# The node stage of a graph layer: one product in its own loop, tokens kept transposed, a written order, first gathers ahead of a branch

## The chip, the core and the metric

The kernel runs on one core of a Trainium2 chip. The core has TensorE (matmuls; PE, its weight loads PEld), VectorE (DVE), ScalarE (ACT) and GpSimd (POOL), which work side by side on on-chip memory (SBUF, and PSUM for the matmuls' sums), and SyncE (SP), which issues transfers. Each engine works through its own queue in order and waits for the others by semaphores. The metric is the device time of one execution in microseconds; lower is better.

## The reference

Two layers work on 6250 nodes of 256 features and 100000 edges. The change lies where layer 0 ends and layer 1 (a graph attention layer) begins. Cut to that:

```python
x = x + processed                                  # layer 0's FFN, for the chosen half of the nodes
xn = layer_norm(layer_norm(x), ln1_g, ln1_b)
h = (xn @ W).reshape(N, HEADS, HEAD_DIM)
a_src = einsum('nhd,hd->nh', h, att_src)
a_dst = einsum('nhd,hd->nh', h, att_dst)
e = leaky_relu(a_src[src] + a_dst[dst], 0.2)
alpha = softmax of e over the edges of each dst
agg = segment_sum(h[src] * alpha[:, :, None], dst)
out = agg.reshape(N, 256) + xn @ W_res + bias
out = layer_norm(out, ln2_g, ln2_b)
...
```

Behind it come a dense FFN of 1024 hidden units and a mixture of eight experts.

## The kernel before

**Tiles.** The 6250 nodes are 50 tiles of 125 (`NT`, `NP`). X, the nodes' features, stays in SBUF for the whole run. Edges are sorted by destination; each node tile has 17 columns of 128 edges (`SL`), in three groups of six, six and five (`GS`).

**The node stage (lines 589 to 695)** runs between layer 0 and layer 1's edges. For every tile:
- `mix` on VectorE adds layer 0's FFN output Y, weighted by wm, to X (L613), and takes mean and variance (bn_stats L177, aggregate L178). `rs` then makes inverse roots for a whole span of tiles by 12 small instructions (L166 to L172); L617 makes the offset. The spans are 1, 2, 2 and then nine times 5 tiles: 12 in all.
- `front`: z = X normalised (ScalarE, L623), two transposes of z on TensorE (L627), and two activations that apply gain and offset and write xT (ScalarE, L629).
- two products of xT on TensorE: with W and the attention vectors into ph, 272 columns (L651), and with W_res into pr, 256 columns (L653).
- three evictions: ht (ScalarE, L654), the attention terms ASAD (VectorE, L655), and rr = pr + bias (VectorE, L656). Per span ht is stored to the table htab and rr to rtab, both in HBM, on SP's queue (L84), and the greatest attention terms of the span go into ext (L660 to L665).

The order of the instructions on each engine is chosen by a scheduler here, which lets instructions of several tiles stand between one another.

**From the stage to the edges.** A few small instructions make one flag of ext (L671 to L692). `nc.values_load(f1I)` (L698) reads it on every engine, and a branch (L699) skips the general path, which these inputs don't need. The load waits for every engine's work and every transfer that is under way. Behind the branch VectorE makes adsh, the destinations' terms in three bf16 parts (L709 to L717). Then the edge part begins: `fetch(s)` gathers a group's rows of htab, one indirect DMA of 128 rows for each column, on GpSimd (L342), into a ring of four buffers, and for a tile's third group SP reads the tile's own rows (L752, L753). `fetch_tile(t)` has SP read the tile's one-hot source ohT (L759, 535 KB) and rr. `load` has SP read expert weights (L146). `onehot_t` compares ohT (VectorE, L766), `spread` multiplies it by adsh (TensorE, L774), and `quarter0` to `quarter3` do a group's softmax weights, the weighted rows and their sum in four quarters; L812 is the first instruction of a group's first quarter. From L723 on, the order on TensorE, VectorE and ScalarE is the program's own, with quarters of the edge work put between the products of FFN and experts of the nodes that are done.

At L1138 the edge part starts with `load(0)`, `load(1)`, `fetch(0)`, `fetch_tile(0)`, `fetch(1)`, `fetch(2)`. GpSimd's only other work here is in `add_o`: L916 adds a constant row to X, 14 times in all, and is placed by the scheduler in the node stage, behind each chunk's last z, since it needs nothing later.

Of the kernel before, what the change touches and what calls it, by code (L numbers as in the profile page):

```python
# [58 lines left out]
def gnn_ffn(ctx, tc, A, out):  # L59
# [529 lines left out]
    w2 = ctx.enter_context(tc.tile_pool(name="w2", bufs=1))  # L589
    with ExitStack() as md:  # L590
# [6 lines left out]
        for t0 in range(0, NT, XC):  # L597
            Y.append(wp.tile([NP, XC, D], F32, name=f"Y{t0}"))
            ndma(Y[-1], ytab, t0, True, eng=(nc.sync, nc.scalar)[(t0 // XC) % 2])
# [5 lines left out]
        MC = 5  # L605
        spans = [(0, 1), (1, 2), (3, 2)] + [(t, MC) for t in range(5, NT, MC)]

        def mix(t0, c):

            mv = pool.tile([NP, MC, 2], F32, name="mv")  # L610
            for j in range(c):
                t = t0 + j
                nc.vector.scalar_tensor_tensor(X[:, t, :], Y[t // XC][:, t % XC, :], wm[:, t:t + 1], X[:, t, :], op0=ALU.mult, op1=ALU.add)  # L613
                bn(pool, mv[:, j, :], X[:, t, :])
            r2 = pool.tile([NP, 2, MC], F32, name="r2", bufs=3)
            rs(pool, r2[:, 0, 0:c], mv[:, 0:c, 1], 1.0 + 1e-5, 1e-10)
            nc.vector.scalar_tensor_tensor(r2[:, 1, 0:c], mv[:, 0:c, 0], -1.0, r2[:, 0, 0:c], op0=ALU.mult, op1=ALU.mult)  # L617
            return r2

        def front(t, r2, j):  # L620

            z = pool.tile([NP, D], F32, name="z")
            nc.scalar.activation(z, X[:, t, :], AF.Identity, bias=r2[:, 1, j:j + 1], scale=r2[:, 0, j:j + 1])  # L623
            pt = psum.tile([P, KD, NP], F32, name="mi", bufs=3)
            xT = pool.tile([P, KD, NP], F32, name="xT", bufs=3)
            for k in range(KD):
                nc.tensor.transpose(pt[:, k, :], z[:, k * P:(k + 1) * P], ident[0:NP, 0:NP])  # L627
            for k in range(KD):
                nc.scalar.activation(xT[:, k, :], pt[:, k, :], AF.Identity, bias=ln1_b[:, k:k + 1], scale=ln1_g[:, k:k + 1])  # L629
            return xT  # L630

        stats = [mix(*spans[0])]
        fronts = []
        for s, (t0, c) in enumerate(spans):
            if s + 1 < len(spans):
                stats.append(mix(*spans[s + 1]))
            if s == 0:
                fronts.append(front(0, stats[0], 0))
            ht = pool.tile([NP, MC, HW], F32, name="ht")
            rr = pool.tile([NP, MC, D], F32, name="rr")  # L640
            for j in range(c):
                t = t0 + j
                if j + 1 < c:
                    fronts.append(front(t + 1, stats[s], j + 1))
                elif t + 1 < NT:
                    fronts.append(front(t + 1, stats[s + 1], 0))
                xT = fronts[t]
                ph = psum.tile([NP, HA], F32, name="ph")
                pr = psum.tile([NP, D], F32, name="pr")
                for k in range(KD):  # L650
                    nc.tensor.matmul(ph, xT[:, k, :], wcat[:, k, 0:HA], start=(k == 0), stop=(k == KD - 1))  # L651
                for k in range(KD):
                    nc.tensor.matmul(pr, xT[:, k, :], wcat[:, k, HA:HA + D], start=(k == 0), stop=(k == KD - 1))  # L653
                nc.scalar.activation(ht[:, j, :], ph[:, 0:HW], AF.Copy)  # L654
                nc.vector.tensor_copy(ASAD[:, t, :], ph[:, D:HA])  # L655
                nc.vector.tensor_tensor(rr[:, j, :], pr, g_bias[0:NP, :], ALU.add)  # L656
            ndma(ht[:, 0:c, :], htab, t0, False)
            ndma(rr[:, 0:c, :], rtab, t0, False)
            e1 = pool.tile([NP, MC, 2 * HEADS], F32, name="e1")
            nc.vector.tensor_copy(e1[:, 0:c, 0:HEADS], ASAD[:, t0:t0 + c, 0:HEADS])  # L660
            nc.vector.tensor_scalar(e1[:, 0:c, HEADS:], ASAD[:, t0:t0 + c, 0:HEADS], -1.0, None, op0=ALU.mult)
            e2 = ext if s == 0 else pool.tile([NP, 2 * HEADS], F32, name="e2")
            nc.vector.tensor_reduce(e2, e1[:, 0:c, :].rearrange("p t h -> p h t"), AX.X, ALU.max)
            if s:
                nc.vector.tensor_tensor(ext, ext, e2, ALU.max)  # L665
# [30 lines left out]

        mid.close()
# [9 lines left out]


        rem = keep.tile([NP, NT, 2 * HEADS], F32, name="rem")  # L709
        for ts in (slice(0, 3), slice(3, NT)):  # L710
            nc.vector.tensor_tensor(shift[:, ts], shift[:, ts], ASAD[:, ts, HEADS:], ALU.add)
            leaky(rem[:, ts, HEADS:], shift[:, ts])
            nc.vector.tensor_copy(rem[:, ts, 0:HEADS], ASAD[:, ts, HEADS:])
            for q in range(3):
                nc.vector.tensor_copy(adsh[0:NP, ts, q, :], rem[:, ts])
                if q < 2:
                    nc.vector.tensor_tensor(rem[:, ts], rem[:, ts], adsh[0:NP, ts, q, :], ALU.subtract)  # L717
# [5 lines left out]
    with ExitStack() as p2:  # L723
        pool = p2.enter_context(tc.tile_pool(name="p2", bufs=2))
        wp = p2.enter_context(tc.tile_pool(name="w3", bufs=1))
        psum = p2.enter_context(tc.tile_pool(name="p2p", bufs=2, space=PSUM))
        p2.enter_context(tc.manual_schedule(engines={mybir.EngineType.PE, mybir.EngineType.DVE, mybir.EngineType.Activation}))

        imin = wp.tile([P, P], F32, name="imin")
        nc.vector.tensor_scalar_min(imin, iota, float(NP))  # L730
        selfT = wp.tile([NP + 1, P], BF16, name="selfT")
        nc.vector.tensor_scalar(selfT, imin[0:NP + 1, :], pcol[0:NP + 1, :], None, op0=ALU.is_equal)
        ring = [wp.tile([P, GS, HW], F32, name=f"hrow{k}") for k in range(4)]
        for r in ring:
            nc.gpsimd.memset(r[:, GS - 1, :], 0.0)
        NG = -(-SL // GS)
        assert NG * GS == SL + 1
        LAST = NT * NG
        live, tiles, outs, ended = {}, {}, {}, set()
        place = {t0 + j: (c, j) for c, (t0, n) in enumerate(CHUNKS1) for j in range(n)}  # L740

        def fetch(s):
            if s >= LAST:
                return
            t, g = divmod(s, NG)
            rows = ring[s % len(ring)]
            live[s] = {"rows": rows}
            for i in range(GS):
                if g * GS + i < SL:
                    gather(rows[:, i, :], htab, srcT[:, t, g * GS + i:g * GS + i + 1])  # L750
                else:
                    nc.sync.dma_start(rows[0:SPLIT, i, :], htab[NP * t:NP * t + SPLIT, :])  # L752
                    nc.sync.dma_start(rows[SPLIT:NP, i, :], htab[NP * t + SPLIT:NP * (t + 1), :])  # L753
# [379 lines left out]
        def ends(ci):  # L1133

            t0, n = CHUNKS1[ci]
            return 4 * NG * (t0 + n) + 3

        load(0, ("W1", "W2", "Wo"))  # L1138
        load(1, ("W1", "W2"))
        fetch(0)  # L1140
        fetch_tile(0)
        for k in range(1, len(ring) - 1):
            fetch(k)
        onehot_t(0)
# [430 lines left out]
```

## Time and profile before

| | us |
|---|---|
| median of 3 runs | 3304.16 (3302.11 to 3304.63) |
| the profiled execution | 3303.96, of which its span 3302.2 |

| row of the page | count | busy us | mean ns |
|---|---|---|---|
| TensorE, L651 (ph) in the node stage | 200 | 56.7 | 406 |
| TensorE, L653 (pr) in the node stage | 200 | 52.3 | 385 |
| ScalarE, L629 (xT) | 100 | 40.0 | 452 |
| GpSimd, L916 | 14 | 29.9 | 2136 |
| ScalarE, L623 (z) | 50 | 29.6 | 593 |
| VectorE, L613 (mix) | 50 | 25.1 | 505 |
| VectorE, L656 (rr) | 50 | 20.7 | 414 |
| VectorE, L177 (bn_stats) | 50 | 20.6 | 416 |
| ScalarE, L654 (ht) | 50 | 19.2 | 384 |
| GpSimd, L342, gathers of htab over the whole run | 850 | 952.7 | 1121 |

These are the groups of instructions between 1258 and 1383 us of the span, and for the last row those of the page. An fp32 product counts twice per contraction half, so 50 tiles make 200 instructions. Busy times of one engine can add up to more than the time, as an instruction begins before the one ahead of it has ended; for what an engine gets through, the distance from start to start is the better number. Idle time of an engine counts only where something waits for it.

### The profile page before, as it was taken

Reading aid. Unit: us, or ns where it says so; the run is one execution under the profiler, and the core shown is the slowest. Engines: PE = TensorE matmul, PEld = TensorE weight load, DVE = VectorE, ACT = ScalarE, POOL = GpSimd, SP = SyncE. Lnnn points to the kernel's source line nnn. Section 1 sums busy time; section 2 is a strip of 40 time slices with the busy share of each in tenths; the row PEclk is TensorE's granted clock in tenths of the full one; section 3 lists DMA queues with packets and bytes.
Section 4 is the critical chain, followed back from the end, with each engine's and each line's share of the span. In section 5 each row is a group of like instructions: output and inputs, shape, how many; then the busy total and the mean of one; then the engine's idle time right before and its main releaser. Section 6 shows DMA issues by size and latency. Waiting matters only on the chain.

```text
span 3302.2 us, 40488 instructions
## 1 busy us (share of the span) xinstructions
PE 2842.7 (86%) x12746; PEld 1981.7 (60%) x12746; DVE 2011.5 (61%) x5670; ACT 1165.6 (35%) x2193; POOL 1857.6 (56%) x1772
## 2 busy tenths in 40 slices
PE   5378889888888996757889999999999999999999
PEld 5245666666666674546666666665666666666665
DVE  8543444444444459578777677767667777766731
ACT  5111212222222224534443534344353434434332
POOL 0277777777777741277665555556555555556300
PEclk8679999999999997979999999999999999999999
DMA  5633343333333426466454454535444454544312
GB/s 106 172 103 111 112 114 111 110 110 112 112 110 112 115 73 158 126 170 187 138 169 131 127 152 118 156 106 151 127 127 140 120 151 120 148 123 134 115 48 64
DMA packets 263978, 412.04 MB, mean 125 GB/s; under 512 B 55450, under 2 KB 202374, under 8 KB 263711
## 3 DMA queue, kind: packets, MB, share of 16 engines
q0 software_dynamic: 81600, 226.41, 24.7%
q1 hardware_dynamic: 169062, 170.03, 17.9%
q10 hardware_dynamic: 13080, 12.80, 1.6%
q8 instruction: 106, 1.74, 0.2%
q14 instruction: 130, 1.06, 0.1%
HBM read 376.61 MB, written 33.24 MB: 124 GB/s over the span
## 4 chain that ended last, share of the span: by engine, by line
PE 29%; DVE 9%; issue 7%; POOL 6%; DMA 3%; ACT 3%; DVEq 0%; POOLq 0%; ACTq 0%
PE ph L1021 14%; PE py L1039 7%; POOL hrow L342 6%; PE py L934 3%; PE iotaP L835 3%; DMA hrow<-htab,sdT 2%; DVE lo L800 2%; DVE hrow L843 1%; DVE ad L812 1%; DVE X L1042 1%; DVE bnst L177 1%; PE ph L923 1%; PE pa L774 1%; PE mi L961 1%; ACT h L1022 1%
## 5 line engine op out<-in xcount | busy, mean ns | idle before, releaser
L342 POOL DMA_INDIRECT hrow<-htab,sdT x850 | 952.7, 1121 | 681.3 <-DVE lo L800 319.9
L342 POOL DMA_INDIRECT rows<-gtab,sdT x850 | 805.7, 948 | 258.5 <-issue 128.6
L404 PE MATMUL ps<-rows,oh 128*125 128x257 f32 x1700 | 479.2, 421 | 76.4 <-DMA rows<-gtab,sdT 62.8
L1022 ACT ACTIVATE h<-ph,bi,sc 128x500 f32<-128x500 f32 (+3 forms) x448 | 322.4, 722 | 600.8 <-PE ph L1021 600.4
L404 PEld LDWEIGHTS ps<-rows,oh 128*125 128x125 f32 x1700 | 326.3, 203 | 218.0 <-DMA rows<-gtab,sdT 130.9
L1021 PE MATMUL ph<-h,W 128*128 128x500 f32 (+3 forms) x896 | 380.3, 557 | 0.6 <-ACT h L1022 0.6
L1021 PE MATMUL ph<-wcat,W 128*128 128x500 f32 (+3 forms) x896 | 373.8, 557 | 0.3
L1039 PE MATMUL py<-Wo,h 128*125 128x256 f32 x1600 | 370.9, 381 | 0.4 <-ACT h L1022 0.4
L800 DVE TENSOR_TENSOR lo<-hrow,hi 128x792 fp32r<-128x792 f32 (+1 forms) x300 | 296.0, 987 | 119.0 <-ACT hi L853 119.0
L1039 PEld LDWEIGHTS py<-Wo,h 128*125 128x125 f32 x1600 | 297.5, 188 | 72.4 <-issue 26.1
L1042 DVE SCALAR_TENSOR_TENSOR X<-py,gate,X 125x256 f32<-125x256 f32 x400 | 174.8, 480 | 221.8 <-PE py L1039 220.3
L843 DVE TENSOR_TENSOR hrow<-hrow 128x768 f32<-128x768 f32 x300 | 273.0, 952 | 32.6 <-ACT hrow L821 32.4
L853 ACT ACTIVATE hi<-hrow 128x792 fp32r<-128x792 f32 (+1 forms) x300 | 232.4, 817 | 144.3 <-DVE hrow L843 144.1
L835 PE MATMUL iotaP<-hi,oh 128*125 128x264 f32 x850 | 252.9, 329 | 0.0
L1021 PEld LDWEIGHTS ph<-wcat,W 128*128 128x128 f32 x896 | 166.2, 198 | 143.3 <-issue 120.1
L835 PE MATMUL iotaP<-lo,oh 128*125 128x264 f32 x850 | 224.1, 295 | 31.3 <-DVE lo L800 31.2
L1021 PEld LDWEIGHTS ph<-h,W 128*128 128x128 f32 x896 | 162.4, 197 | 109.6 <-issue 98.1
L835 PEld LDWEIGHTS iotaP<-lo,oh 128*125 128x125 f32 x850 | 163.5, 192 | 50.8 <-DVE lo L800 37.3
L467 PE MATMUL ph<-xT,f_w 128*128 128x500 f32 (+3 forms) x448 | 189.9, 549 | 0.5 <-ACT xT L457 0.5
L923 PE MATMUL ph<-xT,h_w 128*128 128x500 f32 (+3 forms) x448 | 184.0, 555 | 1.9 <-ACT hT L925 1.0
L476 PE MATMUL py<-f_w,hT 128*125 128x256 f32 x800 | 182.8, 381 | 1.2 <-DVE y L477 0.4
L934 PE MATMUL py<-h_w,hT 128*125 128x256 f32 x800 | 177.6, 380 | 0.0
(305 smaller groups left out, 3706.2 us busy)
## 6 DMA issues: line engine op xcount, KB each, us to landing
W<-in_L_ffn_W SPq DMA_DIRECT2D x224, 256.0 KB
Wo<-in_L_ffn_Wo SPq DMA_DIRECT2D x112, 256.0 KB
ohT<-dltab SPq DMA_DIRECT2D x50, 535.5 KB
rows<-gtab,sdT POOLq DMA_INDIRECT x850, 2.8
hrow<-htab,sdT POOLq DMA_INDIRECT x850, 3.3
hrow<-htab SPq DMA_DIRECT2D x50, 115.5 KB
X<-in_x ACTq DMA_DIRECT2D x10, 560.0 KB
ytab<-y SPq DMA_DIRECT2D x50, 112.0 KB
```

The source lines that it names most:

```text
L342: nc.gpsimd.indirect_dma_start(out=dst, out_offset=None, in_=tab, in_offset=bass.IndirectOffsetOnAxis(ap=idx, axis=0))
L404: nc.tensor.matmul(ps, oh[:, i, :], rows[:, i, :], start=(s0 + i == 0), stop=(s0 + i == SL - 1))
L800: nc.vector.tensor_tensor(L["lo"][:, c], L["rows"][:, c], L["hi"][:, c].bitcast(F32), ALU.subtract)
L835: nc.tensor.matmul(tiles[t]["ps"], L["oh"][:, i, :], r[:, i, :], start=(g + i + q == 0), stop=(g * GS + i == SL - 1 and q == 1))
L843: nc.vector.tensor_tensor(h4, h4, rows[:, c, D:, None].to_broadcast([P, GS // 2, HEADS, HD]), ALU.mult)
L853: nc.scalar.activation(L["hi"][:, c], L["rows"][:, c], AF.Copy)
L923: nc.tensor.matmul(ph[:, 0:n], h_w1[:, k, f * P:(f + 1) * P], C["xT"][:, k, 0:n], start=(k == 0), stop=(k == KD - 1))
L934: nc.tensor.matmul(py[:, i, :], C["hT"][f][:, j * NP:(j + 1) * NP], h_w2[:, f, :], start=(f == 0), stop=(f == NF - 1))
L1021: nc.tensor.matmul(ph[:, 0:n], w[:, k, f * P:(f + 1) * P], rhs[:, k, 0:n], start=(k == 0), stop=(k == KD - 1))
L1022: nc.scalar.activation(h[:, f, 0:n], ph[:, 0:n], AF.Relu, bias=cols[1][:, f, e:e + 1], scale=cols[0][:, f, e:e + 1])
L1039: nc.tensor.matmul(py[:, i, :], hidden[u, "2"][:, k, j * NP:(j + 1) * NP], weights[u, "Wo"][:, k, :], start=(k == 0), stop=(k == KD - 1))
L1042: nc.vector.scalar_tensor_tensor(X[:, t0 + j, :], py[:, i, :], chunk[ci]["gate"][:, j, e:e + 1], X[:, t0 + j, :], op0=ALU.mult, op1=ALU.add)
```

## The change

The node stage is written anew; the rest of the program stays as it is.

- The W_res product leaves the tile's trip and gets a loop of its own behind the table's. For that the transposed tokens of all 50 tiles stay on chip: xT is written over the tile's part of Y, which has been read by then (Y's tiles now have 128 partitions).
- The order on TensorE, VectorE, ScalarE and GpSimd is written out: the trip for tile t does the table product of t, the eviction of t-1, transposes and gain of t+2, the normalising of t+4, and then mixes what the next span needs. Spans are 1, 2, 2, 5 and four times 10 tiles: 8 in all. z of two tiles in five is made by GpSimd.
- ht is evicted with its 16 attention columns, and ASAD is copied from it once for each group of five tiles. The greatest terms are taken over 20, 20, 8 and 2 tiles, as a maximum and a minimum.
- htab is then complete before the W_res loop, and the gathers of the first three groups stand ahead of that loop, and ahead of the branch, on GpSimd. The ring and its constants are made before the stage.
- adsh is made in `terms()`, behind the sixth pair of tiles of the W_res loop, and once more in the branch's general path.
- rr is added for two tiles at a time and stored for four.
- Behind the branch SP first reads ohT and rr of tile 0, then the own rows, then the weights.

```diff
+    def fetch(s):
+        if s < LAST:
+            fetch_edges(s)
+            own_rows(s)
...
-        spans = [(0, 1), (1, 2), (3, 2)] + [(t, MC) for t in range(5, NT, MC)]
...
+        mid.enter_context(tc.manual_schedule(engines={mybir.EngineType.PE, mybir.EngineType.DVE, mybir.EngineType.Activation, mybir.EngineType.Pool}))
+        spans = [(0, 1), (1, 2), (3, 2), (5, 5)] + [(t, 10) for t in range(10, NT, 10)]
+        groups = [(t, 5) for t in range(0, 45, 5)] + [(45, 3), (48, 2)]
...
+        xTs = [Y[t // XC][:, t % XC, 0:KD * NP].rearrange("p (k m) -> p k m", k=KD) for t in range(NT)]
+
+        def mix(t):
...
+            nc.vector.scalar_tensor_tensor(X[:, t, :], Y[t // XC][0:NP, t % XC, :], wm[:, t:t + 1], X[:, t, :], op0=ALU.mult, op1=ALU.add)
+            bn(pool, mv[:, t - t0, :], X[:, t, :])
+            if t == t0 + c - 1:
+                rs(pool, r2[:, 0, 0:c], mv[:, 0:c, 1], 1.0 + 1e-5, 1e-10)
+                nc.vector.scalar_tensor_tensor(r2[:, 1, 0:c], mv[:, 0:c, 0], -1.0, r2[:, 0, 0:c], op0=ALU.mult, op1=ALU.mult)
+
+        def norm(t):
...
+            if t % 5 in (1, 3):
+                nc.gpsimd.tensor_scalar(zs[t], X[:, t, :], r, m, op0=ALU.mult, op1=ALU.add)
+            else:
+                nc.scalar.activation(zs[t], X[:, t, :], AF.Identity, bias=m, scale=r)
...
+        mixed = 0
+        for t in range(-4, NT + 1):
+            u = t + 4
...
+                want = b0 + (u - a0 + 1) * bc // ac
...
+            ph = product(t) if 0 <= t < NT else None
+            if 1 <= t:
+                evict(t - 1, last)
+            last = ph
+            if 0 <= t + 2 < NT:
+                turn(t + 2)
+                gain(t + 2)
+            if u < NT:
+                norm(u)
+            while mixed < want:
+                mix(mixed)
+                mixed += 1
+
+        for k in range(len(ring) - 1):
+            fetch_edges(k)
...
+        for t in range(0, NT, 2):
+            pr = psum.tile([NP, 2, D], F32, name="pr")
+            for i in range(2):
+                for k in range(KD):
+                    nc.tensor.matmul(pr[:, i, :], xTs[t + i][:, k, :], wcat[:, k, HA:HA + D], start=(k == 0), stop=(k == KD - 1))
+            j = t % 4
+            if j == 0:
+                rr = pool.tile([NP, 4, D], F32, name="rr")
+            nc.vector.tensor_tensor(rr[:, j:j + 2, :], pr, g_bias[0:NP, None, :].to_broadcast([NP, 2, D]), ALU.add)
+            if j == 2 or t + 2 == NT:
+                ndma(rr[:, 0:j + 2, :], rtab, t - j, False)
+            if t == 10:
+                terms()
         mid.close()
         gen1 = nc.values_load(f1I[0:1, 0:1], min_val=0, max_val=1)
...
+        fetch_tile(0)
+        for k in range(len(ring) - 1):
+            own_rows(k)
         load(0, ("W1", "W2", "Wo"))
         load(1, ("W1", "W2"))
-        fetch(0)
-        fetch_tile(0)
-        for k in range(1, len(ring) - 1):
-            fetch(k)
         onehot_t(0)
```

`turn`, `gain`, `product` and `evict` hold the transposes, the two xT activations, the two halves of the table product, and the eviction with its store, as before. `terms` holds the lines of L709 to L717 unchanged.

## The prediction

> **What bounds the kernel now.** I read the page first, then the busy time of each engine by stage, then timelines of the stage that the change rewrites. The page's slices show TensorE at nine tenths in the whole second half, so layer 1's edge and expert loop is TensorE's; the chain that ended last stands on it. What the change touches lies between 1259 and 1412 us:
>
> ```profile
> core 0: us, PE busy (x) PEld busy (x) DVE busy (x) ACT busy (x) POOL busy (x), PEclk, DMA share, GB/s
> 1259.00:1270.00 11.00, 1.07 (x4) 0.66 (x5) 10.75 (x59) 1.67 (x4) 0.72 (x1) 0.50 1.11 237
> 1270.00:1340.00 70.00, 62.23 (x287) 49.84 (x286) 69.20 (x330) 46.69 (x118) 17.41 (x8) 0.96 0.35 101
> 1340.00:1383.00 43.00, 42.57 (x212) 35.27 (x210) 17.95 (x65) 31.27 (x80) 11.78 (x5) 1.00 0.41 122
> 1383.00:1391.00 8.00, 0.66 (x3) 0.38 (x3) 2.25 (x12) 0.00 (x0) 0.00 (x0) 0.82 0.58 170
> 1391.00:1412.00 21.00, 0.08 (x2) 0.08 (x3) 6.88 (x15) 0.00 (x0) 13.71 (x14) 0.50 0.75 187
> 1412.00:1470.00 58.00, 31.60 (x186) 27.39 (x187) 43.01 (x102) 23.27 (x42) 44.94 (x40) 0.68 0.49 136
> ```
>
> Until 1340 VectorE is full (10.75 of 11, 69.20 of 70), from 1340 to 1383 TensorE is (42.57 of 43), and from 1383 to 1412 TensorE stands still. So this stage has a VectorE part, a TensorE part and a gap of some 30 us. In the ramp behind it no engine is full; in it every later instruction hangs on the first step of the edges, so what moves that step moves the end.
>
> **Two facts of VectorE decide the first part.** GpSimd's add of a constant (L916) stops it:
>
> ```profile
> 1286.27 2.36 POOL L916 TENSOR_TENSOR X<-X,cst 125x1024 f32<-125x1024 f32 x1 [4.11 <-DVE r L617]
> ...
> 1286.96 1.95 DVE L613 SCALAR_TENSOR_TENSOR X<-Y,wm,X 125x256 f32<-125x256 f32 x1
> ```
>
> L613 takes 0.48 us elsewhere; here it ends with GpSimd's instruction. In eight such adds one VectorE instruction is longer each time, by 1.1 to 2.05 us; for the full width I take 1.74, the mean of six. And an instruction that needs the one before it waits for its end, while an independent one starts before that end:
>
> ```profile
> 1300.34 0.15 DVE L170 SCALAR_TENSOR_TENSOR rsh<-rsy,rsv 125x5 f32<-125x5 f32 x1
> 1300.40 0.48 DVE L613 SCALAR_TENSOR_TENSOR X<-Y,wm,X 125x256 f32<-125x256 f32 x1
> 1300.80 0.16 DVE L171 TENSOR_TENSOR rsh<-rsh,rsy 125x5 f32<-125x5 f32 x1
> ...
> 1435.40 0.43 DVE L177 BATCH_NORM_STATS2 bnst<-o 125x6 f32<-125x256 f32 x1
> 1435.86 0.18 DVE L178 BATCH_NORM_AGGREGATE mv<-bnst 125x2 f32<-125x6 f32 x1
> 1436.08 0.15 DVE L166 TENSOR_SCALAR rsv<-mv 125x1 f32<-125x1 f32 x1
> ```
>
> At 1300, where several tiles' instructions are interleaved, the small L170 costs 0.06 us of start to start and L613 0.40. At 1435, in a dependent row, bn_stats costs 0.46, the aggregate 0.22, and the 12 instructions of a root 2.31 us (1436.08 to 1438.39), 0.19 each.
>
> **The first loop (transposes, table product, eviction).** TensorE gets 50 x (0.22 + 0.92) = 57 us instead of 100: at 1375, start to start, a tile's two transposes take 0.22, its table product 0.92, its W_res product 0.86. ScalarE needs per tile 0.69 for two xT, 0.29 for ht, 0.49 for z on three tiles of five: 1.27, or 63 us. VectorE loses the rr adds but is now in written order, where tile after tile is mixed, summed and aggregated:
> - 50 mixes x (0.52 + 0.46 + 0.10) = 54 us. 0.52 is L613's 0.48 and the 0.04 between dependent instructions; 0.10 because the next mix doesn't need the aggregate.
> - 8 root chains (there are 8 spans now, 12 before) x (2.31 + 0.19) = 20 us.
> - GpSimd. Eleven of the 14 adds fall while VectorE still mixes, which runs ten to fourteen tiles ahead: 8 x 1.74 + 3 for the three narrow ones = 17 us. In the table's first three rows they already cost like this.
> - GpSimd's 20 new z instructions, 16 of them in this time. No row shows tensor_scalar on GpSimd. Between a one-input cast of half the width (0.28 us) and the add of 125x256 (0.72) I take 0.5. Costless for VectorE if it never meets one; 11.5 at 0.72 met in full; I take 3, since a z often falls beside bn_stats, which the trace shows running through an add (L177 at 1286.22).
> - The ASAD copies, now per group, and the reductions: 2 us. They stand in VectorE's queue behind ScalarE's eviction; before, ASAD's copy waited 23.1 us for ht in all, mostly when VectorE had nothing else. I add 3 for such waits.
>
> Together 99 us. The last span (tiles 40 to 49) can be normalised only then; from its first z to the last product there are 13 trips at ScalarE's 1.27 and a product of 1.08: 17.6. The first loop ends 117 us behind 1259.25, at 1376. ScalarE's own sum of 63 and TensorE's 57 hide under it.
>
> **Two rules of the Trainium skill, weighed.** "VectorE: DVE Perf Modes", section "The DRAIN you can't avoid", says that leaving out the semaphores between chained operations gains nothing, as the pipe drains either way. If a dependence cost nothing, written order would keep before's pace: 50 x (0.40 + 0.33 + 0.09) + 8 x 13 x 0.07 = 48 us instead of 74, and VectorE's sum would be 73, level with ScalarE. The rows at 1300 and 1435 show a difference, 0.06 against 0.19; I go by them, and the rule is a rival below. "SBUF — State Buffer", section "Who interferes with whom", speaks against moving z to GpSimd: a VectorE instruction with two SBUF inputs and a GpSimd one that reads SBUF exclude each other for the whole instruction. By that the 16 z cost 8 us, by overlap as in the adds' rows 3.
>
> **Between the loops** TensorE's queue holds the maximum's transpose and the broadcast product ahead of the W_res loop. Before, from the last ht (1381.74) to that product's end (1384.97) it took 3.2 us; it was part of the gap, and now stands between the loops: 3.2 us.
>
> **The second loop** is 50 x 0.86 = 43 us of TensorE; VectorE's adds (25 of double width, about 0.7 each) hide under it. terms() stands in VectorE's queue behind the adds of tiles 10 and 11; before it took 6.1 us (1391.1 to 1397.2), in written order with its small slice first about 7. With two PSUM buffers TensorE runs two pairs on, 3.4 us, and then waits: 7 + two adds less 3.4 = 5. Ends at both sides: 0 and 8. The 17 gathers take 17 x 1.25 = 21 us of GpSimd, at most 29 at the 1.7 of the ramp, and are hidden here; so are the stores, 26 of rtab instead of 24, on SP. Second loop: 48 us, TensorE done at 1376 + 3 + 48 = 1427, against 1382.6 before: **44 us later**.
>
> **The branch and the first step.** Before:
>
> ```profile
> 1391.10 0.64 DVE L711 TENSOR_TENSOR shift<-shift,ASAD 125x24 f32<-125x24 f32 x2 [4.80 <-SPq L699]
> ...
> 1399.82 0.46 SPq L759 DMA_DIRECT2D ohT<-dltab  x1
> ...
> 1411.08 0.79 DVE L766 TENSOR_SCALAR ohT<-ohT,pcol 126x2176 bf16<-126x2176 bf16 x1 [13.88 <-DMA rr<-rtab]
> ...
> 1412.38 0.46 DVE L812 TENSOR_REDUCE ad<-pa 128x96 f32<-128x288 f32 x1 [0.52 <-PE pa L774]
> ```
>
> The last rr ended at 1383.2 and the engines go on at 1391.1: 7.9 us for its store (the branch waits for every transfer) and the flag. That stays; the store is 224 KB instead of 625, so 7.4, behind the last add's 0.8. Then before spent 21.3 us to the first step (1412.38): terms, after which five weights went first on SP (1397.33), then ohT, under a full DMA. Now ohT is SP's first transfer: 0.9 us to issue, landing estimated at 4.7 (535 KB at the 265 GB/s seen from 1400 to 1410 is 2.0, and 2.7 like a gather's fixed part), onehot 0.8, spread 0.5: 6.9 us. First step at 1427 + 0.8 + 7.4 + 6.9 = 1442, against 1412.4: **29.7 us later.** The weights, now behind ohT, are used only 50 us on.
>
> The gathers themselves shorten the ramp no more: group 3's rows landed about 1428 and were used at 1430.8, and later groups had 8 us and more, so they weren't late; the ramp is VectorE's and ScalarE's small steps in turn. From the first step on nothing changes.
>
> **Sum.** 3303.96 (the profiled execution's time; its span is 3302.2) + 29.7 = 3333.7. The median shown is 3304.16, 0.2 above: I say 3333.
>
> **Rivals.**
> - *Written order costs VectorE nothing* (10%), the other side. VectorE's sum is 73, the first loop 75, bounded by ScalarE after a start of 10.8: the first step falls at 1400, and the time is 3292. It decides once the first loop is under 87 us. For it: the skill's rule, and TensorE's freed 43 us. Against it: the 0.19 of the chains.
> - *GpSimd's z is slow* (15%): at 2 us each, 24 us more of GpSimd, two thirds of it met by VectorE: +16, 3349. For it: a form that the trace doesn't show. Against: adds of twice the inputs take 0.72.
> - *The gathers did hold the ramp* (15%): GpSimd works from 1394 to 1469 with hardly a gap. Then its head start counts in full, 21.3 + 3.2 for its late first gather = 24.5 instead of 14.4: 3323. Against it: the rows' spare time above.
> - The forecast, 60%, own range 3318 to 3350.
>
> That the gathers don't come before the branch is excluded as far as the queue goes: they are GpSimd's next instructions behind the last add, and need only the table's last store.
>
> **How the numbers follow.** 3308 to 3352 takes in the forecast and the middle rivals with their unknown costs (z 0 to 16, terms -5 to +3, ohT's landing 2 either way), and leaves out the fast one and what lies beyond slow z. A difference of 0.2% is 6.6 us, about what can be told from no change. Faster by more: 0.09, the fast rival less its slow edge. Within: 0.04. Slower: 0.87.
>
> **What would show it.** In the changed profile: VectorE full for about 97 us from 1259 with TensorE at half in it; mix, bn_stats and aggregate at 1.08 us a tile; L916's successor lengthening an instruction by 1.7; TensorE full for 43 us with one hole of 5; 6 to 8 us from the branch to the first L812. It is wrong if the first loop takes under 87 us, or if the ramp from the first step to 1470's state is 10 us shorter.

## The result, and the profile after

| | us |
|---|---|
| before, median of 4 runs | 3303.14 (3299.86 to 3304.63) |
| after, median of 4 runs | 3331.75 (3327.15 to 3334.95) |
| ratio, 95% interval | 1.0087 [1.0069, 1.0104] |
| after, the profiled execution | 3333.41, of which its span 3331.6 |

The change makes the kernel 0.9% slower. 3333 was predicted. The busy times by stage, in the columns of the table shown for before (the end of the first loop, from 1353 to 1380 us, and the ramp are left out):

```profile
core 0: us, PE busy (x) PEld busy (x) DVE busy (x) ACT busy (x) POOL busy (x), PEclk, DMA share, GB/s
1261.00:1272.00 11.00, 1.49 (x5) 1.10 (x6) 9.69 (x42) 2.09 (x5) 2.23 (x3) 0.50 1.11 234
1272.00:1353.00 81.00, 55.56 (x217) 39.97 (x216) 67.95 (x210) 48.02 (x128) 30.66 (x25) 0.83 0.19 57
...
1380.00:1433.00 53.00, 46.77 (x202) 39.52 (x201) 25.52 (x48) 0.00 (x0) 16.70 (x17) 0.94 0.53 154
1433.00:1445.00 12.00, 0.34 (x6) 0.33 (x7) 0.97 (x2) 0.00 (x0) 4.76 (x5) 0.65 0.63 178
```

While VectorE mixes (to 1353), TensorE is busy for 55.56 of 81 us, where before it had 62.23 of 70. Note that VectorE's busy share is only 84% here, although it sets the pace: busy time leaves out the gap that a dependent instruction waits for, and the waits for ht that come up below. Then comes a W_res loop of 53 us, 47 of it TensorE's, and a gap of 12 us before the edges instead of some 29.

VectorE's timeline in the first loop shows the written order, one tile after the other, 1.05 us from mix to mix:

```profile
1277.02 0.45 DVE L652 SCALAR_TENSOR_TENSOR X<-Y,wm,X 125x256 f32<-125x256 f32 x1
1277.51 0.43 DVE L177 BATCH_NORM_STATS2 bnst<-X 125x6 f32<-125x256 f32 x1
1277.97 0.18 DVE L178 BATCH_NORM_AGGREGATE mv<-bnst 125x2 f32<-125x6 f32 x1
1278.07 0.45 DVE L652 SCALAR_TENSOR_TENSOR X<-Y,wm,X 125x256 f32<-125x256 f32 x1
```

The hole in the W_res loop, and the way from the branch to the first step, in the timeline:

```profile
1380.08 14.08 PE L783 MATMUL pr<-wcat,Y 128*125 128x256 f32 x64
...
1390.75 0.69 DVE L787 TENSOR_TENSOR rr<-pr,g_bias 125x512 f32<-125x512 f32 x1 [1.03 <-PE pr L783]
...
1398.26 0.94 DVE L773 CAST adsh<-rem 125x752 bf16<-125x752 f32 x1
1399.11 1.28 DVE L787 TENSOR_TENSOR rr<-pr,g_bias 125x512 f32<-125x512 f32 x2
1399.85 4.63 PE L783 MATMUL pr<-wcat,Y 128*125 128x256 f32 x10 [5.69 <-DVE rr L787]
...
1438.66 0.34 SPq L819 DMA_DIRECT2D ohT<-dltab  x1
...
1445.12 0.46 DVE L872 TENSOR_REDUCE ad<-pa 128x96 f32<-128x288 f32 x1 [0.52 <-PE pa L834]
```

Between the adds at 1390.75 and 1399.11 stands terms(), without a gap (its last instruction is the one at 1398.26); TensorE, two pairs ahead, waits 5.69 us for the add. The wait has a second price. Behind it TensorE runs for a few us at half its clock (PEclk):

```profile
core 0: us, PE busy (x) PEld busy (x) DVE busy (x) ACT busy (x) POOL busy (x), PEclk, DMA share, GB/s
1380.00:1394.00 14.00, 14.00 (x66) 12.00 (x65) 7.74 (x24) 0.00 (x0) 9.73 (x11) 1.00 0.63 178
1400.00:1403.00 3.00, 3.00 (x8) 2.33 (x9) 0.39 (x1) 0.00 (x0) 2.19 (x3) 0.50 0.70 212
1407.00:1411.00 4.00, 4.00 (x20) 3.47 (x20) 1.67 (x3) 0.00 (x0) 0.00 (x0) 1.00 0.44 128
```

In the record of the granted clock the 0.50 lasts from 1399.1 to 1405.9. A matmul of this product takes 0.43 us of start to start there and 0.22 elsewhere, so about 14 of them cost 3 us more. The first step (L872, the L812 of before) comes at 1445.12, 32.7 us later than before. With stage boundaries read off the timelines:

| | before | after |
|---|---|---|
| first mix | 1259.25 | 1261.63 |
| first mix to last mix | 75.3 | 91.2 |
| first mix to last ht (first loop) | 122.9 | 116.1 |
| last ht to last rr | 1.1 | 55.5 |
| last rr to first step | 29.2 | 11.9 |
| first step to end of span | 1889.8 | 1886.5 |

The whole difference of 29.4 us in the span comes out of this table: +2.4 in the start, -6.8, +54.4, -17.3 and -3.3. The start is nothing of the change's: in all six profiles of A in the section below, before and after among them, the code up to there is the same but for the set-up of the gathers' ring, and the first mix lies between 1258.0 and 1261.9. The -3.3 can't be told from nothing: behind the first step e_inter, e_adds and after run the same code, and take 1883.6 to 1886.6 us, and e_act, after_again and e_terms take 1888.4 to 1894.8. The ramp itself, from the first step to that of the seventh group of edges, takes 57.6 us before and 57.0 after.

### The profile page after: what moved, and what is told of

It is laid out like the page before. It is cut to its first block, busy times and chain, and to the rows that moved or that the text cites. A ratio compares the mean times of both kernels' runs of the same rounds, so it can differ in the third digit from the quotient of the medians.

```text
span 3331.6 us, 40322 instructions
## 1 busy us (share of the span) xinstructions
PE 2863.4 (86%) x12746; PEld 1991.4 (60%) x12746; DVE 2013.7 (60%) x5522; ACT 1153.3 (35%) x2173; POOL 1867.2 (56%) x1792
## 4 chain that ended last, share of the span: by engine, by line
PE 29%; DVE 9%; issue 7%; POOL 6%; ACT 3%; DMA 2%; DVEq 0%; SPq 0%; POOLq 0%; ACTq 0%
PE ph L1081 14%; PE py L1099 7%; POOL hrow L342 6%; PE py L994 3%; PE iotaP L895 3%; DMA hrow<-htab,sdT 2%; DVE lo L860 2%; DVE hrow L903 1%; DVE X L1102 1%; DVE ad L872 1%; PE ph L983 1%; DVE bnst L177 1%; ACT hi L913 1%; PE mi L1021 1%; ACT h L1082 1%
## 5 line engine op out<-in xcount | busy, mean ns | idle before, releaser
L404 PE MATMUL ps<-rows,oh 128*125 128x257 f32 x1700 | 486.2, 425 | 76.2 <-DMA rows<-gtab,sdT 62.1
```

What stands on the lines that cost most here:

```text
L404: nc.tensor.matmul(ps, oh[:, i, :], rows[:, i, :], start=(s0 + i == 0), stop=(s0 + i == SL - 1))
```

## The experiments

All stage lengths, in us. Before and after above belong to A, where the kernel before takes some 3301 us. B was taken elsewhere, in two batches: there the kernel before takes 3712 us (the first three and e_sched) and 3708 us, and the difference lies in layer 0, since the first mix comes at 1647 to 1671 while the stages behind it, the W_res loop apart, are about as long as in A. A ratio compares with the kernel before of the same batch.

The traces show one more difference, and it bears on every reading from B in the W_res loop. In B some products of TensorE are signalled later than the profile's model has them done, and VectorE or ScalarE waits. The profile puts such a wait down to "remote", since no instruction's modelled end stands beside it; the semaphore that ends it is TensorE's each time. In layer 0 these waits sum to 616 to 678 us in the eight profiles of B, at VectorE's adds of the W_res loop to 2.1 to 13.3 us; in the six of A there are none. Whether the product or its signal is late, and why in B alone, stays open; B's traces also lack many records of signals and landings.

| run | first to last mix | first loop | last ht to last rr | to first step | rest | ratio, interval |
|---|---|---|---|---|---|---|
| A: e_inter | 78.8 | 108.4 | 57.2 | 11.2 | 1883.6 | 1.0069 [1.0055, 1.0083] |
| A: e_adds | 83.2 | 106.1 | 57.0 | 11.4 | 1886.6 | 1.0064 [1.0051, 1.0078] |
| A: e_late | 90.8 | 115.4 | 55.6 | 11.6 | 1894.1 | 1.0120 [1.0105, 1.0135] |
| A: b_sp | 74.8 | 122.4 | 1.1 | 21.6 | 1893.4 | 0.9998 [0.9990, 1.0007] |
| B: e_all | 72.2 | 101.2 | 87.3 | 11.0 | 1890.1 | 1.0086 [1.0055, 1.0117] |
| B: e_terms | 91.0 | 115.6 | 58.9 | 11.4 | 1894.8 | 1.0066 [1.0045, 1.0087] |
| B: e_act | 96.9 | 120.9 | 61.2 | 11.5 | 1888.4 | 1.0062 [1.0038, 1.0086] |
| B: e_sched | 60.8 | 95.5 | 45.1 | 12.0 | 1888.3 | 0.9970 [0.9957, 0.9982] |
| B: after_again | 91.0 | 115.6 | 61.4 | 11.6 | 1890.0 | 1.0071 [1.0045, 1.0098] |
| B: e_schedc | 47.9 | 79.8 | 46.8 | 11.3 | 1928.3 | 1.0054 [1.0034, 1.0074] |
| B: e_fuse28 | 64.0 | 102.6 | 32.3 | 11.1 | 1884.7 | 0.9971 [0.9956, 0.9987] |
| B: e_fuse28c | 52.8 | 95.7 | 35.3 | 11.6 | 1932.7 | 1.0057 [1.0037, 1.0076] |

### VectorE's order alone (e_inter)

```diff
-            bn(pool, mv[:, t - t0, :], X[:, t, :])
-            if t == t0 + c - 1:
-                rs(pool, r2[:, 0, 0:c], mv[:, 0:c, 1], 1.0 + 1e-5, 1e-10)
...
+            chain(1)
+            for f, s in ((take, t - 1), (mean, t - 2)):
+                if s in sums:
+                    f(s)
+                    chain(1)
...
+            if u >= 5:
+                want = min(NT, want + min(u - 4, 5))
```

take is bn_stats, mean the aggregate, and chain(1) emits the next instruction of a root that is under way; `want` makes mixing run up to five tiles further ahead.

> The changed kernel, with VectorE's order in the first loop interleaved: from tile 10 on bn_stats of the tile before and the aggregate of the one before that stand between the mixes, and the instructions of a root stand between those of the next span's tiles (for which mixing runs up to five tiles further ahead). Same instructions, same amounts. My theory (an instruction that needs the one ahead of it waits for its end): 40 tiles x (1.05 - 0.82) = 9 us and four chains of which 9 of 13 instructions find cover, 36 x 0.12 = 4 us; the first loop goes from 115.5 us to 102, the time from 3332 to about 3319, 1.005 of the kernel before. Rival (the pipe drains between instructions whether they depend or not): first loop 115, time 3332, 1.0087.

VectorE's timeline of e_inter, where a root (L684 to L697) stands between tiles, and a line from where it doesn't run:

```profile
1306.40 0.48 DVE L652 SCALAR_TENSOR_TENSOR X<-Y,wm,X 125x256 f32<-125x256 f32 x1
1306.80 0.16 DVE L686 TENSOR_SCALAR rsy<-rsv 125x10 int32<-125x10 int32 x1
1306.87 0.42 DVE L672 BATCH_NORM_STATS2 bnst<-X 125x6 f32<-125x256 f32 x1
1307.21 0.15 DVE L688 TENSOR_SCALAR rsy<-rsy 125x10 int32<-125x10 int32 x1
...
1310.40 0.24 DVE L749 COPY ASAD<-ht 125x80 f32<-125x80 f32 x1 [1.75 <-ACT ht L746]
1310.56 1.34 DVE L652 SCALAR_TENSOR_TENSOR X<-Y,wm,X 125x256 f32<-125x256 f32 x1
```

The same instructions start 0.40, 0.07 and 0.34 us apart, where after has 0.49, 0.19 (in a chain) and 0.46. The last mix comes 12.4 us earlier, 13 were expected. Some 2 us of it aren't the order's, since GpSimd's adds happen to lengthen the mixes less (31.4 us in sum instead of 33.3); running further ahead saves nothing by itself, as VectorE's only gaps up to the last mix, the waits below, don't shrink. With some 10 us left for it the mechanism holds, and its size nearly. The first loop gains only 7.7 us and the time by ratio about 6 (0.0018 of 3300, with intervals that overlap). What took the rest is in the last two lines. The written order puts ASAD's copy into VectorE's queue, where it waits for ScalarE's ht, and every mix behind it with it. Before the last mix such waits sum to 7.4 us in after and 8.2 in e_inter; VectorE is ahead of ScalarE now, and ScalarE doesn't go faster. In e_inter's tail ScalarE runs like this:

```profile
1349.96 0.80 ACT L723 ACTIVATE Y<-mi,ln_bc,ln_gc 128x125 f32<-128x125 f32 x2 [0.51 <-PE mi L718]
...
1353.03 0.80 ACT L723 ACTIVATE Y<-mi,ln_bc,ln_gc 128x125 f32<-128x125 f32 x2 [0.51 <-PE mi L718]
```

Two tiles take 3.07 us, 1.53 each, and in each such round ScalarE waits 0.51 us for TensorE's transposes.

### The constant's adds out of the first loop (e_adds)

```diff
         for k in range(len(ring) - 1):
             fetch_edges(k)
+        for t0, n in CHUNKS1:
+            nc.gpsimd.tensor_tensor(X[:, t0:t0 + n, :], X[:, t0:t0 + n, :], cst[0:NP, None, :].to_broadcast([NP, n, D]), ALU.add)
...
-            nc.gpsimd.tensor_tensor(X[:, t0:t0 + n, :], X[:, t0:t0 + n, :], cst[0:NP, None, :].to_broadcast(bc), ALU.add)
```

> The changed kernel, with GpSimd's 14 adds of the constant row put behind its gathers, into the W_res loop, where VectorE has half its time free. My theory (each add stops VectorE for about 1.7 us): no mix over 0.6 us is left beside an add, the first loop goes from 115.5 us to about 100, nothing comes back in the W_res loop, and the time is about 3317 (1.004). Rival (the adds fall where VectorE would wait anyway, for z's readers or for ht): first loop 112 to 115, time 3329 to 3332. A third: the same stop comes back in the W_res loop, which then goes from 52 to over 60 us, and the sum stays at 3332.

The group of the 50 mixes, between 1258 and 1380 us; first after, then e_adds (busy time, mean ns):

```profile
L652 DVE SCALAR_TENSOR_TENSOR X<-Y,wm,X 125x256 f32<-125x256 f32 x50 | 33.3, 665 | 0.1
```

```profile
L652 DVE SCALAR_TENSOR_TENSOR X<-Y,wm,X 125x256 f32<-125x256 f32 x50 | 23.8, 476 | 0.1
```

The adds lengthen the mixes by 9.5 us and one small instruction of a root by 2.0 (2.20 us instead of 0.17, at 1333.99 in after), and nothing else on VectorE by much. The last mix comes 8.0 us earlier, as the waits for ht grow from 7.4 to 9.9 us; the first loop ends 10.0 us earlier. Expected were 15. So the adds do stop VectorE, for 11.5 us, not the 17 of the prediction, and the first loop pays 10 for it. They don't come back in the W_res loop (57.0 against 55.5), though they run there back to back for 29 us beside it: rr reads one operand from PSUM.

### The gathers behind the branch again (e_late)

```diff
-        for k in range(len(ring) - 1):
-            fetch_edges(k)
...
         for k in range(len(ring) - 1):
-            own_rows(k)
+            fetch(k)
```

> The changed kernel, with the first 17 gathers behind the branch again, after ohT and rr of the first tile on SP's queue, as the kernel before has them in GpSimd's. My theory (the gathers matter only for the first group): its six gathers take 7.5 us and land 2.7 later, so the first step comes 10 to 11 us behind the branch instead of 6.5, and the time goes from 3332 to 3336 (1.010). Rival (the gathers hold the whole ramp): the head start of 17 x 1.25 = 21 us is lost in full, less what the branch hid: +14 or more, 3346 (1.013).

The timeline behind the branch in e_late:

```profile
1437.34 1.01 POOL L342 DMA_INDIRECT hrow<-htab,sdT  x1 [62.86 <-SPq L792]
...
1443.67 0.46 DVE L870 TENSOR_REDUCE ad<-pa 128x96 f32<-128x288 f32 x1 [0.51 <-PE pa L832]
...
1450.86 0.21 DVE L872 TENSOR_TENSOR w<-hrow,ad 128x48 f32<-128x48 f32 x1 [6.73 <-DMA hrow<-htab,sdT]
```

The first step is where it was (11.6 us behind the last rr), since it reads no gathered row; the instruction behind it does, and waits 6.73 us. The expectation's marker was badly chosen: it had the first step move. The groups behind follow later still: the seventh group's first step comes 68.2 us behind the first, against 57.0 in after. The rest of the profiled execution is 7.6 us longer, which alone is no more than this stretch scatters over A and B, but the seventh group is 11.2 us later, and by the ratios, whose intervals don't overlap, the time is 11 us longer. The early gathers are worth some 11 us, between my 4 and the rival's 14.

### The kernel before with the new order on SP alone (b_sp)

```diff
-        load(0, ("W1", "W2", "Wo"))
-        load(1, ("W1", "W2"))
-        fetch(0)
-        fetch_tile(0)
-        for k in range(1, len(ring) - 1):
+        fetch_tile(0)
+        for k in range(len(ring) - 1):
             fetch(k)
+        load(0, ("W1", "W2", "Wo"))
+        load(1, ("W1", "W2"))
```

> The kernel before, with one part of the change: behind the branch SP first reads ohT and rr of the first tile, then come the gathers and their own rows, and the five weights last. My theory: the first step then hangs on the terms (6 us), the six gathers (7.5 and 2.7 to land) and spread, 12 to 14 us behind the branch instead of 21.3; the time goes from 3303 to about 3296 (0.998). Rival (the gathers hold the ramp): the first step is earlier, but the groups behind it wait for their rows and the time stays at 3303 (1.000).

The first step comes 7.6 us earlier, and the time doesn't move (0.9998): my theory falls. The timeline of b_sp shows the first group's and the fourth group's use of gathered rows, and the fourth's last gather:

```profile
1411.03 0.21 DVE L814 TENSOR_TENSOR w<-hrow,ad 128x48 f32<-128x48 f32 x1 [3.52 <-DMA hrow<-htab,sdT]
...
1429.36 0.95 POOL L342 DMA_INDIRECT hrow<-htab,sdT  x1 [0.30 <-issue]
...
1432.40 0.21 DVE L814 TENSOR_TENSOR w<-hrow,ad 128x48 f32<-128x48 f32 x1 [2.90 <-issue]
```

The first waits 3.52 us for its rows; the fourth starts 3.0 us behind the issue of its last gather, after an idle 2.90 us that the profile puts down to nothing else. GpSimd gathers without a gap there, 1.25 us from one to the next at the least and up to 1.9, six for a group. The seventh group begins 86.8 us behind the last rr in b_sp (21.6 + 65.2) and 86.8 in before (29.2 + 57.6): the same point, however early the first step was. Neither part works alone. SP's order without early gathers brings nothing, and early gathers need a first step that is early too; together they bring the ramp forward by 86.8 - 68.9 = 17.9 us.

### terms() spread out (e_terms), z (e_act), three edits together (e_all)

In e_terms terms() is a generator, and one instruction of it stands behind each pair:

```diff
-            if t == 10:
-                terms()
+            if t >= 10:
+                next(parts, None)
```

> The changed kernel, with the instructions of terms() spread over the pairs of the W_res loop, one behind each pair from the sixth on, instead of all of them behind the sixth. My theory (TensorE's hole of 5.7 us is terms() ahead of the next add in VectorE's queue): the hole is gone, the second loop goes from 53 to 48 us, the time from 3330 to 3325 (1.007). Rival (the branch waits for something else that ends at the same time, such as the stores): no change, 1.0087.

From last ht to last rr it takes 58.9 us, against 61.4 in after_again; the ratios differ by less than their intervals. The hole is not gone, it has another cause. The timeline of e_terms, and the DMA queues' packets between 1794.9 and 1801.5 us:

```profile
1776.08 14.04 PE L788 MATMUL pr<-wcat,Y 128*125 128x256 f32 x56
...
1799.91 0.69 DVE L792 TENSOR_TENSOR rr<-pr,g_bias 125x512 f32<-125x512 f32 x1 [9.08 <-remote]
...
q0 software_dynamic: 211, 0.57, 31.8%
```

The add, the seventh, waits 9.08 us, and TensorE stands behind it for 7.87; there are three such waits, 12.0 us in all, up to 1801; the 17 gathers run from 1777 to 1799. A free rr buffer, of which there are two, is not what the add waits for: VectorE's waits for the store of that buffer are recorded as over at 1790.09 and 1790.19, and in the last 5 us of the wait no packet moves but the gathers' (q0) and one of instructions; the stores go on q1. What comes last is TensorE's signal, at 1799.89, though by the profile's model the seven pairs up to this one are done at 1790.12. So the run met B's late signals, and its theory was not tested. The W_res loop of after_again is longer than A's before its seventh add, by 6.2 us, most of it waits for such signals.

In after itself no signal is late. There the product of the seventh pair was done at 1392.45 and the buffer's store had landed at 1391.85, and VectorE was in terms() until 1399.11: the hole of A is terms(), and what spreading it out would save in A was not tried. The stores don't crawl either: beside the gathers a store of four tiles (500 KB) lands 3.8 to 4.8 us after its issue in after, and 3.4 us when the gathers are over.

e_act makes all z on ScalarE (`if t % 5 in ()`).

> The changed kernel, with all 50 z on ScalarE, none on GpSimd. My theory (GpSimd's z at 0.66 us hardly stop VectorE; ScalarE has room while VectorE bounds, and needs 0.2 us more a tile in the last 13 trips): first loop 115 to 119 us, time 3329 to 3333 (1.0085 to 1.0095). Rival (a z and a VectorE instruction of two inputs exclude each other in full, 16 x 0.66 less what falls on gaps): VectorE gains 8 us, first loop 110, 3323 (1.007).

The first loop grows by 5.3 us against after_again, the time doesn't move beyond its interval. So z on GpSimd takes hardly anything of VectorE: the rival falls. e_adds shows it directly, as there no add is in the way: 16 mixes that met a z took 0.51 us on average, the other 34 took 0.46, which makes 0.9 us in all. The last mix comes 5.9 us later with all z on ScalarE. The mixes take 36.8 us in sum instead of 34.5, all of it beside GpSimd's adds, and the waits for ht 8.4 us instead of 6.4; why the adds fall on the mixes more was not followed up.

e_all is e_inter, e_adds and e_terms in one.

> The changed kernel with three edits together: VectorE's interleaved order, the constant row's adds behind the gathers, and the instructions of terms() spread over the pairs of the W_res loop, one behind each pair from the sixth on. By the runs before, the interleaving brought the last mix 12 us forward and the adds 8. My theory (VectorE's losses add up, and under them lies ScalarE's and TensorE's trip of about 1.5 us a tile): last mix some 71 us behind the first, first loop 92 to 96 us, second loop 48 instead of 53 to 55, time about 3304 (1.001). Rival (the two savings overlap, or the trip of ScalarE and TensorE holds the loop already at 106): time about 3317 (1.005).

The last mix comes at 72.2, as the sum of the two edits says; the first loop ends at 101.2, not 94, for VectorE now waits 13.3 us for ht at ASAD's copies. And the W_res loop is 26 us longer than in after_again. Two waits for late signals stand in it (5.54 and 7.78 us), and then this, in GpSimd's and VectorE's timeline:

```profile
1784.07 28.95 POOL L785 TENSOR_TENSOR X<-X,cst 125x256 f32<-125x256 f32 x14
...
1787.63 25.43 DVE L822 TENSOR_TENSOR shift<-shift,ASAD 125x24 f32<-125x24 f32 x1
```

An add of 24 columns on VectorE takes 0.17 us in after and 25.43 here: it has two operands in SBUF, and GpSimd runs its 14 adds of two SBUF operands back to back. It ends with the last of them (1813.06 and 1813.02), and TensorE waits 22 us for the add behind it. This is my edit's fault: in e_adds terms() was over before the adds began.

### Without the written order (e_sched), and what follows from it

```diff
-        mid.enter_context(tc.manual_schedule(engines={mybir.EngineType.PE, mybir.EngineType.DVE, mybir.EngineType.Activation, mybir.EngineType.Pool}))
```

> The changed kernel without its written order: the scheduler orders the four engines as in the kernel before. It interleaves VectorE's instructions of several tiles, and puts some 8 of the 25 pairs of the W_res product among the table's products. My theory (the written order is what cost VectorE its cover): the last mix falls near 80 us behind the first instead of 91; the first loop takes about 110 us with 8 adds of rr in it, the second 53 - 14 = 39; time about 3310 (1.003). Rival (VectorE's loss is GpSimd's alone, or the order was no loss): first loop 116 plus the 8 adds, second 39, time 3325 to 3330 (1.007 to 1.0087).

This line alone turns 1.0071 (after_again) into 0.997, some 37 us. The last mix comes at 60.8 instead of 91.0, and no copy of ASAD waits before it: the scheduler interleaves the tiles, as e_inter did, puts each copy where its ht is done, and mixes further ahead. From VectorE's timeline:

```profile
1677.21 0.48 DVE L651 SCALAR_TENSOR_TENSOR X<-Y,wm,X 125x256 f32<-125x256 f32 x1
1677.61 0.16 DVE L171 TENSOR_TENSOR rsh<-rsh,rsy 125x10 f32<-125x10 f32 x1
1677.69 0.48 DVE L651 SCALAR_TENSOR_TENSOR X<-Y,wm,X 125x256 f32<-125x256 f32 x1
```

A part of the W_res product moves into the first loop, which even so ends 20 us earlier. My theory's sign was right and its sum (3310) too small a gain. It left out the waits in the queue, 6.4 us in after_again; what the other things that the scheduler does at once are worth, each by itself, was not tried.

Three more runs were to find a better version. after_again is the changed kernel, beside them.

> The changed kernel itself once more, beside the next three, so that they can be compared on one chip. First mix to last ht 116 us, from there to the last add of rr 55, first step 12 behind it, 1.0087 of the kernel before.

It agrees, but for the W_res loop, which is 6 us longer than in A, mostly by late signals (see e_terms).

e_schedc is e_sched with the constant added to o, behind o's gain, instead of to X:

```diff
-            nc.gpsimd.tensor_tensor(X[:, t0:t0 + n, :], X[:, t0:t0 + n, :], cst[0:NP, None, :].to_broadcast(bc), ALU.add)
+            nc.gpsimd.tensor_tensor(o[:, 0:n, :], o[:, 0:n, :], cst[0:NP, None, :].to_broadcast(bc), ALU.add)
```

> The changed kernel without its written order, and the constant row added to o behind its gain instead of to X, so that GpSimd can't do its 14 adds before the edges' output is there. My theory (the adds still cost VectorE some 6 us in the first loop, but there ScalarE and TensorE bound now; in the edge part TensorE bounds): mixes at 0.48 us, first loop 92 to 95 us, edge part unchanged at 1888, ratio 0.995 to 0.998. Rival (GpSimd's gathers are close behind their use in the edge part, so 30 us of adds there hold them up): edge part 1895 to 1910, ratio 1.000 to 1.005.

The first loop takes 79.8 us, the shortest of all, with the last mix at 47.9: without the adds VectorE gains 12.9 more. And the rest takes 1928.3, 40 us more, so the rival is right and was too small. The groups of VectorE's weights behind the first step show where a part of it arises; first e_sched, then e_schedc (busy time, mean ns):

```profile
L873 DVE TENSOR_TENSOR w<-hrow,ad 128x48 f32<-128x48 f32 x150 | 31.3, 209 | 5.2
```

```profile
L873 DVE TENSOR_TENSOR w<-hrow,ad 128x48 f32<-128x48 f32 x150 | 49.4, 329 | 5.2
```

The 14 adds stop this small instruction for 18 us, and TensorE's wait for lo, which comes after it, grows from 31.0 to 49.3 us. The other half wasn't followed up; 14 us of it lie in one product of the FFN (TensorE, L982, 198.1 us instead of 183.9), and why is open. The adds' place in the node stage, which costs 10 us of first loop in e_adds and 15.7 here, is the cheaper one.

e_fuse28 is e_sched with three rr buffers, where the first 28 tiles' W_res product is made in the table's loop, a pair behind every second tile:

```diff
+            if t % 2 == 1 and 0 < t < 28:
+                residual(t - 1)
```

> The changed kernel without its written order, with the W_res product of the first 28 tiles in the table's loop again, and only the last 22 tiles' product (11 pairs, 19 us) behind it, over the gathers; three rr buffers instead of two. My theory (TensorE stood half idle in the first loop, and only some 20 us of work are needed to cover the gathers): first mix to last ht about 105 us, 20 to 24 from there to the last rr, so the first step falls some 14 us earlier than without the written order alone; ratio 0.992 to 0.994. Rival (the rr adds take VectorE what TensorE gains, or the branch now waits for the gathers): no gain over the scheduler alone, 0.997.

Last rr falls 134.9 us behind the first mix, against 140.6 in e_sched: 5.7 us earlier, not 14, and the ratio is the same, 0.9971. Its W_res rest takes 32.3 us instead of 20 to 24, of which two rr adds wait 11.9 us on what the trace calls remote. As in e_terms that is TensorE's signal (the second add's waits for a buffer are over at 1777.46, and it starts at 1786.54), so a third rr buffer could not help. Without the two waits it would be some 20, as expected; whether A, without late signals, gets that was not run. e_fuse28c adds the constant to o as well.

> The same, with the constant row added to o as well. My theory: VectorE bounds the first loop again (mixes, 14 and more pairs of rr adds), so freeing it of the adds brings 5 us: ratio 0.990 to 0.993. Rival (the edge part pays for the adds): the edge part over 1895 us, ratio 0.995 or more.

It pays for it in the edge part like e_schedc (1932.7), and the rival is right again.

So e_sched and e_fuse28 are 0.3% faster than before, and 1% faster than after, in B; in A they weren't run.

## Why the prediction was right

By its own steps, with what each measured (after, in A, unless said otherwise):

- **VectorE bounds the first loop, 117 us: 116.1.** A tile costs 1.05 us for 1.08, a root to the next mix 2.6 for 2.5. e_inter shows that the dependence is the cause: same instructions, other order, last mix 12.4 us earlier, some 10 of them by the order. This is also where the Trainium skill's "VectorE: DVE Perf Modes", section "The DRAIN you can't avoid", was weighed against the rows; the rival drawn from it (10%, 3292) falls with e_inter. That is against the rival and not against the section, which also says that a next instruction that is not held starts earlier, as the small ones do in e_inter.
- **The adds, 17: 11.5.** Mis-sized. Of the eleven adds nine lengthen a mix and one an instruction of a root; 1.74 for each was too much, as an add often falls in part beside bn_stats. Waits for ht, 3: 7.4 before the last mix. z, 3: under 1, though one takes 0.66 us and not 0.5. These three make 23 by the prediction and some 20 by the measurement.
- **The last span, 17.6 behind VectorE's last root: 20.1** (the root ends at 95.9, ht at 116.1). The trip was 1.53 us, not ScalarE's own 1.27, as ScalarE waits for TensorE's transposes. The error cancels against the one above (VectorE's sum 95.9 for 99), so that 116 came out of a sum whose terms were off by 2 to 6. That is luck.
- **Between the loops 3.2: 2.4.**
- **The W_res loop, 48, and the last add, 0.8: 53.1** from the first product to the last rr. 25 pairs at 1.727 are 43.2. The hole itself was sized well, TensorE waits 5.69 us for the 5 that were forecast. What the sum had at nothing is the half clock behind it, some 3 us. e_terms could not show what spreading terms() saves, since B's late signals stand in its place.
- **Branch and first step, 14.3: 11.9**: 5.5 from the last rr to SP's first transfer, for 7.4, and 6.5 from there, for 6.9.
- **The ramp unchanged: 57.0 us for 57.6.** The reason given, that the gathers weren't late, was true of before and no reason for after. b_sp shows that the gathers are the limit as soon as the first step is moved forward, and e_late that the ramp is some 11 us longer without their head start. The size was right because the change moved both, and by a reason that the prediction did not have. The rival that gave the gathers 10 us more than that falls.

The sum was 29.7 for the first step; without the 2.4 of the start it came out at 30.4.

What the change was worth by parts: the ramp gains some 18 us by the gathers, by terms() ahead of the branch and by ohT ahead of the weights. Taking W_res out of the loop costs TensorE 43 us for which VectorE would have to give back the same, and under the written order the first loop gives back 7. Under the scheduler's order it gives back 27 (95.5 in B against 122.9 in A), with some pairs of W_res in it.

## What to carry to other kernels

Before an order is written by hand for an engine, count what the scheduler's interleaving hides: 0.12 us for each dependent small instruction and 0.23 for each tile here, and look in the queue for every instruction that waits for another engine, since all behind it wait too. Work that is taken out of one loop pays only if the loop's own bound falls by as much. And a first step that comes early brings only what the transfers behind it can follow: move both, or neither.

## What the hardware showed that I had not expected

- A VectorE instruction with two SBUF operands can wait for a whole row of GpSimd instructions, not for one: in e_all 25.43 us for 24 columns beside 14 adds of 28.95 us in sum, the one time that a trace has this. rr, with one operand in PSUM, kept its 0.69 us beside the same adds in e_adds. The Trainium skill's "SBUF — State Buffer", section "Who interferes with whom", has such a pair exclude each other for the whole instruction, and says that a VectorE instruction with at most one SBUF input is free of it outside some fast modes. The adds agree with the first and rr with the second. Beside z, which reads SBUF too, the mixes lost only 0.05 us each on average (e_adds), as most z began while a mix was under way.
- TensorE was granted half its clock behind a short wait: 5.69 us of standing still, and 0.50 for 6.8 us (after, 1399.1 to 1405.9).
- A product of TensorE can be signalled 9.8 us behind its modelled end (e_terms, 1790.12 and 1799.89), in B alone; the cause is open.
